# Seven block products instead of eight for the products with A, the last step of LayerNorm on ScalarE, and eight groups in flight

## The chip, the cores and the metric

The kernel runs on one core of one Trainium2 chip. The metric is the device time of one execution in microseconds (us), the median of several runs.

A core has TensorE (PE, matrix products; its weight loads are shown as PEld), VectorE (DVE), ScalarE (ACT), GpSimd (POOL) and a queue that issues DMAs (SP). The engines work side by side, each in its own order, and wait for one another through semaphores. Matrix products read SBUF and write PSUM, of which the kernel uses eight banks of 128 x 512 f32 numbers.

## The reference

x is 64 batches of 256 nodes with 128 features, and A a dense 256 x 256 matrix, all in f32. Four layers run one after another, each as LN(x + layer(x)); LN has no scale or shift.

```python
# layer 0: y = sum over k of X_k W_k with X = x, Ax, AAx, AAAx, Ax, AAx, AAAx
# layer 1: A (x W) + b
# layer 2: An x W^T + b,   An = D^-1/2 (A + I) D^-1/2
# layer 3: five steps of a gated unit
m_in = jnp.einsum('nm,bmd->bnd', in_matrix, h)      # in_matrix = out_matrix = A
z = jax.nn.sigmoid(av @ w3_w.T + w3_b + u3)         # av = [A h, A h]
r = jax.nn.sigmoid(av @ w4_w.T + w4_b + u3)         # u3 = h @ u3_w.T + u3_b
hv = jnp.tanh(av @ w5_w.T + w5_b + (r * h @ u5_w.T + u5_b))
h = (1.0 - z) * h + z * hv
```

## The kernel before

**Tiling.** Two batches make a group (`NB = 2`): 31 groups of two and two groups of one batch at the end (`ONES`). A group's x is one tile of 128 x 512: for each of two batches two node tiles of 128, and 128 features for each. A group runs through all four layers by itself; nothing passes between groups.

**Products with A.** `propagate` (L457) computes h^T A^T for one group: for each batch and each half of the nodes one matmul of 128 x 128 (h, stationary) with 128 x 256 (a row half of A^T), four matmuls in one bank, and then ScalarE copies the bank into SBUF (`copied`, L417). It is called for layer 0 with AA (`q`, bank pmq), for layers 1 and 2 (bank pm) and for each of the five steps (bank pmg). In steps 1 to 4 h comes back through DRAM in another layout (`packed`, `pair_of`).

**LayerNorm.** `statistics` (L422): four BN statistics on VectorE, four aggregations, variance + eps (ve), and one GpSimd operation for the power -1/2 (rs). `normalise` (L446): VectorE computes (s - mean) * rs for each of the four 128-wide parts. For layers 1 and 2 GpSimd adds the bias to y (yb, L595).

**Order.** The kernel writes no order by hand. Each `Group.add` hands an operation with an engine, a cost, a lag and a rank to `Plan`; `Plan.order` (L80) lays all of them out by a greedy list schedule over costs, in which an operation takes its place when its inputs and its slots (banks, SBUF tiles, DRAM buffers) are expected to be free, and among those that can start first the one of the lowest rank. The rank is the group's number; for the last `LEVEL` groups the ranks lie close together and grow with the operation's place in the group. The result is a fixed instruction order for each engine. `ACTIVE` is how many groups may be under way: a group's operations come after the last one of the group `ACTIVE` places ahead of it. Costs decide nothing but the order; what waits on the chip is decided by the real times.

**Start.** `WARM` transposes of the identity run on TensorE until A has arrived. A is transposed, squared, and normalised for layer 2; weights are summed and transposed. The first `HEAD` batches are transposed by TensorE, all later ones by a VectorE block transpose and a way through DRAM (tx, dx, xT).

```python
def propagate(self, tag, h, aTs, ins=None, outs=None):
    ...
            for b in range(self.nb):
                for kt in range(T):
                    mm(o[b], a(h, b * T + kt), aTs.ap[:, kt, :], kt == 0, kt == T - 1)
    ...
    return self.copied("m" + tag, ps)
```

Of the kernel before, what the change touches and what calls it, by code (L numbers as in the profile page):

```python
# [8 lines left out]
F32 = mybir.dt.float32  # L9
AF = mybir.ActivationFunctionType  # L10
# [5 lines left out]
ACTIVE = 6  # L16
HEAD = 4
LEVEL = 6
END = 8
STEPS = 5  # L20
WARM = 12
# [5 lines left out]
class Val:  # L27
# [3 lines left out]
    def __init__(self, kind, shape, name, nb=NB):  # L31
        self.kind, self.shape, self.name, self.nb = kind, shape, name, nb
        self.writer, self.readers, self.users = None, [], []
        self.slot = self.tile = None
# [15 lines left out]
class Plan:  # L50
# [9 lines left out]
    def add(self, engine, cost, lag, rank, run, reads=(), writes=(), after=()):  # L60
        if engine == "SP":
            lag += 700
        op = Op(len(self.ops), rank, engine, cost, lag, run, [*reads, *writes])
        op.deps.update(after)
        for v in reads:
            op.deps.add(v.writer)
            v.readers.append(op)
        for v in writes:
            if v.writer is not None:
                op.deps.add(v.writer)  # L70
            op.deps.update(v.readers)
            v.writer, v.readers = op, []
        op.deps.discard(op)
        for v in op.vals:
            if op not in v.users:
                v.users.append(op)
        self.ops.append(op)
        return op
# [66 lines left out]
def dve_cost(elements):  # L145
    return elements / 0.96 + 75


def act_cost(elements):
    return elements / 1.2 + 165  # L150
# [3 lines left out]
def kernel(  # L154
# [42 lines left out]
    SHAPES = {"bank": [P, 512], "x": [P, 512], "w": [P, 512], "st": [P, Q * 6], "mv": [P, Q * 2],  # L197
              "ve": [P, Q], "rs": [P, Q]}
    slots = {"bank": BANKS, "x": ACTIVE + 3, "w": 54, "dram1": 8, "dram2": 16, "st": 8, "mv": 8, "ve": 8, "rs": 8}
# [3 lines left out]
    def constant(name, shape):  # L203
        v = Val("const", shape, name)
        v.tile = const.tile(shape, F32, name=name)
        return v
# [8 lines left out]
    def load(rank, name, shape, src):  # L215
        v = constant(name, shape)
        pre(rank, "SP", 450, lambda: nc.sync.dma_start(v.ap, src), [], [v])
        return v
# [11 lines left out]
    def warmed():  # L230
        for i in range(WARM):
            nc.tensor.transpose(warm.ap[:, (i % 4) * P:(i % 4 + 1) * P], ident, ident)  # L232
# [4 lines left out]
    a_nat = load(-9, "a_nat", [P, T, N], adj.rearrange("(t p) m -> p t m", p=P))  # L237
# [12 lines left out]
    pre(-8, "PE", 4 * 110, lambda: turn(p_at, a_nat), [a_nat], [p_at])  # L250
# [42 lines left out]
    ahat, anT = constant("ahat", [P, T, N]), constant("anT", [P, T, N])  # L293
# [24 lines left out]


    w1s = load(1.3, "w1s", [P, C], w1)  # L320
    b1s = load(1.4, "b1s", [P, C], bass.AP(tensor=b1.tensor, offset=b1.offset, ap=[[0, P], [1, C]]))
    raw = {name: load(1.5, f"raw_{name}", [P, src.shape[1]], src)
           for name, src in (("w2", w2), ("w4", w4_w), ("w3", w3_w), ("w5", w5_w), ("u3", u3_w), ("u5", u5_w))}
    b2s = load(1.5, "b2s", [P, C], bass.AP(tensor=b2.tensor, offset=b2.offset, ap=[[0, P], [1, C]]))
    both = {name: constant(f"both_{name}", [P, C]) for name in ("w4", "w3", "w5", "w34")}
# [32 lines left out]
    def nat(v):  # L358
        return v.ap.rearrange("p (q c) -> p q c", c=C)
# [7 lines left out]
    def tile_of(v, q):  # L367
        return nat(v)[:, q, :]

    def pair_of(v, q):  # L370
        return v.ap.rearrange("p (b c t) -> p b t c", c=C, t=T)[:, q // T, q % T, :]
# [8 lines left out]
    class Group:  # L380
# [15 lines left out]
        def rank(self):  # L396
            g = self.start / NB
            return g if g < G - LEVEL else G - LEVEL + (g - G + LEVEL) / 10 + self.count / 100

        def add(self, engine, cost, lag, run, reads=(), writes=()):  # L400
            after = () if self.first else self.gate
            self.count += 1
            op = plan.add(engine, cost, lag, self.rank(), run, reads, writes, after)
            self.first = self.first or op
            self.last = op
            return op

        def pe(self, cost, run, reads, writes):
            return self.add("PE", cost, 260, run, reads, writes)

        def dve(self, run, reads, writes, cost=None):
            return self.add("DVE", cost or dve_cost(self.width), 260, run, reads, writes)

        def act(self, run, reads, writes, cost=None):
            return self.add("ACT", cost or act_cost(self.width), 130, run, reads, writes)
# [6 lines left out]
        def statistics(self, tag, s):  # L422
            st, mv, ve, rs = (self.val(k, k + tag) for k in ("st", "mv", "ve", "rs"))

            def stats():
                for q in range(self.q):
                    nc.vector.bn_stats(st.ap[:, q * 6:(q + 1) * 6], nat(s)[:, q, :])  # L427

            def aggr():
                for q in range(self.q):  # L430
                    nc.vector.bn_aggr(mv.ap[:, 2 * q:2 * q + 2], st.ap[:, q * 6:(q + 1) * 6])  # L431
                nc.vector.tensor_scalar(ve.ap, mv.ap.rearrange("p (q k) -> p q k", k=2)[:, :, 1], EPS,  # L432
                                        None, op0=OP.add)

            self.dve(stats, [s], [st], 195 * self.q)
            self.dve(aggr, [st], [mv, ve], 67 * self.q + 142)
            self.add("POOL", 1010, 100,
                     lambda: nc.gpsimd.tensor_tensor(rs.ap, ve.ap, half[:, :self.q], op=OP.pow), [ve], [rs])  # L438
            return mv, rs
# [6 lines left out]
        def normalise(self, tag, s, mv, rs):  # L446
            y = self.val("w", "y" + tag)

            def run():
                for q in range(self.q):  # L450
                    nc.vector.tensor_scalar(nat(y)[:, q, :], nat(s)[:, q, :], mv.ap[:, 2 * q:2 * q + 1],  # L451
                                            rs.ap[:, q:q + 1], op0=OP.subtract, op1=OP.mult)

            self.dve(run, [s, mv, rs], [y], 257 * self.q)
            return y

        def propagate(self, tag, h, aTs, ins=None, outs=None):  # L457

            ps = self.val("bank", "pm" + tag)

            def run():
                o, a = (outs or plain)(ps), ins or tile_of
                for b in range(self.nb):
                    for kt in range(T):
                        mm(o[b], a(h, b * T + kt), aTs.ap[:, kt, :], kt == 0, kt == T - 1)

            self.pe(pe_cost(N, self.q), run, [h, aTs], [ps])
            return self.copied("m" + tag, ps)

# [62 lines left out]
        def record(self):  # L532
# [23 lines left out]
            qT = self.propagate("q", x_, a2T)  # L556
# [3 lines left out]
            for t in range(T):  # L560
                p = self.val("bank", f"py0{t}")
                py.append(p)

                def first(p=p, t=t):
                    for b in range(self.nb):
                        o, q = p.ap[:, b * 2 * C:(b + 1) * 2 * C], b * T + t
                        mm(o, (tile_of if near else pair_of)(xT, q), w01.ap[:, 0:2, :], b == 0, True, shared=True)
                        mm(o, tile_of(qT, q), w0s.ap[:, 2:4, :], False, True, shared=True)

                def moved(p=p, t=t):  # L570
                    nc.scalar.copy(parts(v)[:, t], four(p)[:, :, 1, :])

                self.pe(pe_cost(2 * C, 2 * self.nb), first, [xT, qT, w01, w0s], [p])
                self.act(moved, [p], [v], act_cost(self.nb * C))
            for t in range(T):

                def second(p=py[t], t=t):
                    for kt in range(T):
                        mm(four(p)[:, :, 0, :], aT.ap[:, kt, t * P:(t + 1) * P], parts(v)[:, kt],
                           False, True, shared=True)  # L580

                def summed(p=py[t], t=t):
                    nc.vector.tensor_copy(nat(s0).rearrange("p (b t) c -> p t b c", t=T)[:, t],
                                          four(p)[:, :, 0, :])

                self.pe(pe_cost(self.nb * C, T), second, [v, aT], [py[t]])
                self.dve(summed, [py[t]], [s0], dve_cost(self.nb * C))
# [25 lines left out]
            for s in range(STEPS):  # L613
                m = self.propagate(f"g{s}", h, ats, ins, by_block)
# [14 lines left out]
                if s < STEPS - 1:  # L629
                    hT = self.tensor(f"hT{s}", OP.add, hT, e)  # L630
                    h, ats, ins = self.packed(f"h{s}", hT), aTp, pair_of
# [31 lines left out]
    with tc.manual_schedule():  # L663
        for op in plan.order():
            for v in op.vals:
                if v.tile is None:
                    pool = {"bank": psum_b, "dram1": dram, "dram2": dram}.get(v.kind, sbuf)
                    v.tile = pool.tile(v.shape, F32, tag=f"{v.kind}{v.slot}", name=v.name)
            op.run()
# [30 lines left out]
```

## Time and profile before

| | |
|---|---|
| median of 3 runs | 1382.38 us (1381.41 to 1382.77) |
| profiled execution: its own time / its span | 1382.45 us / 1380.7 us |
| TensorE clock granted, mean over the span | 0.998 |
| matmul passes / VectorE / ScalarE / GpSimd instructions | 5044 / 2735 / 833 / 205 |
| DMA | 134.08 MB, mean 97 GB/s |

The span runs from the first to the last instruction of the profiled execution. "Busy" counts the time in which an engine has at least one operation under way. An f32 matmul stands in the profile as two matmul records (two passes), each with its own weight load. Matmuls overlap with the next one, so a record's length is more than the time that it holds the engine. A group of instructions is named by line, engine and operation, and by what it writes and reads (out<-in).

### The profile page before, as it was taken

The numbers are of one execution on the slowest core, as the hardware profiler recorded it, in microseconds if no ns is written. First come the engines' busy times: TensorE is split into PE (matmuls) and PEld (weight loads), VectorE is DVE, ScalarE is ACT, GpSimd is POOL, SyncE is SP. The second block draws the span as 40 slices with busy tenths as digits, with TensorE's granted clock in tenths as the row PEclk, the third lists the DMA queues.
The fourth block names the chain that finished last, engine by engine and source line by source line (L and its number), as shares of the span: only waits on it lengthen the run. The fifth ranks groups of instructions, "written<-read, shape, count | busy, mean of one in ns | idle before, by whom it ended". The sixth has DMA issues, their size and how long they took to land.

```text
span 1380.7 us, 16602 instructions
## 1 busy us (share of the span) xinstructions
PE 1366.5 (99%) x5044; PEld 922.5 (67%) x5044; DVE 970.5 (70%) x2735; ACT 513.1 (37%) x833; POOL 236.1 (17%) x205
## 2 busy tenths in 40 slices
PE   9999999999999999999999999999999999999996
PEld 8866666666667766566676666667666677766664
DVE  4755686867667767776686767668685778875577
ACT  2233433333433233433424333442334332334443
POOL 1400021202111211011121211012221113210001
PEclk9999999999999999999999999999999999999999
DMA  6023233333333332343241334333232432233332
GB/s 177 31 77 91 85 115 115 91 98 105 112 107 90 109 92 75 97 137 110 64 137 54 108 108 117 95 92 106 78 107 84 118 97 85 85 92 90 86 103 65
DMA packets 271112, 134.08 MB, mean 97 GB/s; under 512 B 177584, under 2 KB 243632, under 8 KB 271024
## 3 DMA queue, kind: packets, MB, share of 16 engines
q1 hardware_dynamic: 271024, 133.03, 33.2%
q8 instruction: 40, 0.66, 0.2%
q14 instruction: 48, 0.39, 0.1%
HBM read 67.05 MB, written 65.54 MB: 96 GB/s over the span
## 4 chain that ended last, share of the span: by engine, by line
PE 97%; DVE 2%; DMA 0%; ACT 0%; issue 0%; POOL 0%; SPq 0%; POOLq 0%; DVEq 0%
PE pr L195 30%; PE ph L195 19%; PE pmg L195 19%; PE py L195 16%; PE pm L195 8%; PE pmq L195 4%; DVE y L451 1%; DMA h<-dh 0%; DVE st L427 0%; PE p_a L195 0%; PE warm L232 0%; DVE s L443 0%; DVE d L529 0%; DVE mv L431 0%; DVE e L529 0%
## 5 line engine op out<-in xcount | busy, mean ns | idle before, releaser
L195 PE MATMUL pr<-mg,w435u5T 128*128 128x512 f32 (+1 forms) x660 | 323.3, 580 | 1.7 <-ACT mg L419 1.4
L438 POOL TENSOR_TENSOR rs<-ve,half 128x4 f32<-128x4 f32 (+1 forms) x132 | 137.9, 1049 | 1049.8 <-DVE ve L432 1049.7
L529 DVE TENSOR_TENSOR d<-hv,hT 128x512 f32<-128x512 f32 (+1 forms) x165 | 113.6, 690 | 189.6 <-ACT hv L522 189.2
L195 PE MATMUL pmg<-aTp,h 128*128 128x256 f32 x1024 | 241.7, 379 | 0.4 <-DMA h<-dh 0.4
L195 PEld LDWEIGHTS pmg<-aTp,h 128*128 128x128 f32 x1024 | 200.4, 196 | 50.5 <-issue 24.4
L529 DVE TENSOR_TENSOR rh<-r,hT 128x512 f32<-128x512 f32 (+1 forms) x165 | 116.5, 706 | 128.2 <-ACT r L522 126.9
L195 PEld LDWEIGHTS pr<-mg,w435u5T 128*128 128x128 f32 x660 | 123.6, 190 | 101.0 <-issue 90.4
L419 ACT COPY mg<-pmg 128x512 f32<-128x512 f32 (+1 forms) x165 | 94.6, 573 | 257.0 <-PE pmg L195 236.5
L451 DVE TENSOR_SCALAR y<-s,mv,rs 128x128 f32<-128x128 f32 x512 | 149.7, 357 | 34.0 <-POOL rs L438 32.5
L195 PE MATMUL pr<-hT,w2u3T 128*128 128x512 f32 (+1 forms) x330 | 163.1, 580 | 1.1 <-DVE hT L529 1.1
L522 ACT ACTIVATE z<-pr,bsum 128x512 f32<-128x512 f32 (+1 forms) x165 | 111.3, 674 | 142.2 <-PE pr L195 137.4
L195 PE MATMUL ph<-mg,w435u5T 128*128 128x512 f32 (+1 forms) x330 | 163.4, 579 | 0.0
L195 PE MATMUL ph<-rh,w435u5T 128*128 128x512 f32 (+1 forms) x330 | 163.0, 579 | 0.0
L522 ACT ACTIVATE r<-pr,bsum 128x512 f32<-128x512 f32 (+1 forms) x165 | 111.3, 674 | 135.2 <-PE pr L195 132.7
L522 ACT ACTIVATE hv<-ph,bsum 128x512 f32<-128x512 f32 (+1 forms) x165 | 111.3, 674 | 53.0 <-PE ph L195 50.9
L529 DVE TENSOR_TENSOR e<-z,d 128x512 f32<-128x512 f32 (+1 forms) x165 | 113.8, 691 | 2.5
L529 DVE TENSOR_TENSOR hT<-hT,e 128x512 f32<-128x512 f32 (+1 forms) x165 | 113.1, 687 | 2.5
L427 DVE BATCH_NORM_STATS2 st<-s 128x6 f32<-128x128 f32 x512 | 109.7, 277 | 0.8
L195 PEld LDWEIGHTS ph<-rh,w435u5T 128*128 128x128 f32 x330 | 62.4, 190 | 69.3 <-issue 59.5
L195 PEld LDWEIGHTS ph<-mg,w435u5T 128*128 128x128 f32 x330 | 62.4, 190 | 67.5 <-issue 54.8
L504 DVE STREAM_TRANSPOSE th<-hT 128x512 f32<-128x512 f32 x132 | 91.0, 689 | 2.0
L195 PEld LDWEIGHTS pr<-hT,w2u3T 128*128 128x128 f32 x330 | 61.6, 190 | 42.0 <-issue 25.2
(79 smaller groups left out, 1373.7 us busy)
## 6 DMA issues: line engine op xcount, KB each, us to landing
dh<-th SPq DMA_DIRECT2D x155, 256.0 KB, 2.0
h<-dh SPq DMA_DIRECT2D x256, 128.0 KB, 2.5
x<-in_x_dram SPq DMA_DIRECT2D x31, 256.0 KB, 3.3
hT<-dh SPq DMA_DIRECT2D x124, 64.0 KB, 2.0
out_dram<-y SPq DMA_DIRECT2D x31, 256.0 KB, 2.4
xT<-dx SPq DMA_DIRECT2D x60, 128.0 KB, 2.5
dx<-tx SPq DMA_DIRECT2D x29, 256.0 KB, 2.6
dn<-tn SPq DMA_DIRECT2D x28, 256.0 KB, 2.0
```

Source lines behind the costliest of these rows:

```text
L195: nc.tensor.matmul(o, lhsT, rhs, start=start, stop=stop, skip_group_check=shared)
L419: self.act(lambda: nc.scalar.copy(t.ap, ps.ap), [ps], [t])
L427: nc.vector.bn_stats(st.ap[:, q * 6:(q + 1) * 6], nat(s)[:, q, :])
L438: lambda: nc.gpsimd.tensor_tensor(rs.ap, ve.ap, half[:, :self.q], op=OP.pow), [ve], [rs])
L451: nc.vector.tensor_scalar(nat(y)[:, q, :], nat(s)[:, q, :], mv.ap[:, 2 * q:2 * q + 1], rs.ap[:, q:q + 1], op0=OP.subtract, op1=OP.mult)
L504: self.dve(lambda: nc.vector.transpose(turn.ap.rearrange("p (u j t) -> p u t j", t=T, j=32), src.ap.rearrange("p (u t i) -> p u t i", t=T, ...
L522: self.act(lambda: nc.scalar.activation(t.ap, ps.ap, func, bias=bias[1], scale=1.0), [ps, bias[0]], [t], act_cost(self.width) + 100)
L529: self.dve(lambda: nc.vector.tensor_tensor(out(t), way(a), way(b), op=op), [a, b], [t])
```

## The change

- **Seven block products.** With h of two batches taken as a 2 x 2 matrix of 128 x 128 blocks (batch by node half), and A^T as another one, `propagate` now calls `seven` for all full groups before the last `PLAIN` = 10 batches, but not for layer 0 of the first two groups and not for steps 1 to 4. `seven` forms three sums of h's blocks on GpSimd (ts, two operations, and tq, one), does seven matmuls of 128 x 128 in four pieces (`first`, `middle`, `more`, `rest`), and puts the result together with a copy of one block by ScalarE (`kept`), three VectorE additions, another copy by ScalarE and one more VectorE addition. The sums of A^T's blocks are made once at the start (`block_sums`, three times five VectorE operations).
- **LN.** The last step is four ScalarE activations, Identity with scale rs and bias -mean * rs; VectorE makes -mean (nm), and GpSimd a second small operation for the product. Layer 0's sum out of PSUM (s0) goes from VectorE to ScalarE.
- **Order.** `ACTIVE` 6 to 8, `LEVEL` 6 to 4, the rank's growth within a group doubled, more slots (w 54 to 60, and others), some constants moved into the shared slots. VectorE costs in the plan are 6% higher. Several operations may now write one value without being ordered among themselves (`joint`).
- **Start.** `WARM` 12 to 14, and four more warming transposes behind those of A.

```diff
-ACTIVE = 6
+ACTIVE = 8
-LEVEL = 6
+LEVEL = 4
+PLAIN = 10
-WARM = 12
+WARM = 14
...
 def dve_cost(elements):
-    return elements / 0.96 + 75
+    return (elements / 0.96 + 75) * 1.06
...
+    def turned_early():
+        turn(p_at, a_nat)
+        warming(4)
...
+        def run():
+            nc.vector.tensor_add(v.ap[:, 0, :], a21, a22)
+            nc.vector.tensor_sub(v.ap[:, 1, :], v.ap[:, 0, :], a11)
+            nc.vector.tensor_sub(v.ap[:, 2, :], a11, a21)
+            nc.vector.tensor_sub(v.ap[:, 3, :], a12, v.ap[:, 1, :])
+            nc.vector.tensor_scalar(v.ap[:, 4, :], a22, -1.0, None, op0=OP.mult)
...
-            return g if g < G - LEVEL else G - LEVEL + (g - G + LEVEL) / 10 + self.count / 100
+            return g if g < G - LEVEL else G - LEVEL + (g - G + LEVEL) / 10 + self.count / 50
...
+                nc.vector.tensor_scalar(nm.ap, mean, -1.0, None, op0=OP.mult)
+
+            def scales():
+                nc.gpsimd.tensor_tensor(rs.ap, ve.ap, half[:, :self.q], op=OP.pow)
+                nc.gpsimd.tensor_tensor(mv.ap[:, :self.q], nm.ap, rs.ap, op=OP.mult)
...
-                    nc.vector.tensor_scalar(nat(y)[:, q, :], nat(s)[:, q, :], mv.ap[:, 2 * q:2 * q + 1],
-                                            rs.ap[:, q:q + 1], op0=OP.subtract, op1=OP.mult)
-
-            self.dve(run, [s, mv, rs], [y], 257 * self.q)
+                    nc.scalar.activation(nat(y)[:, q, :], nat(s)[:, q, :], AF.Identity, bias=mv.ap[:, q:q + 1],
+                                         scale=rs.ap[:, q:q + 1])
+
+            self.act(run, [s, mv, rs], [y], 400 * self.q)
...
+            if fast and self.nb == 2 and self.start < B - PLAIN:
+                return self.seven(tag, h, aTs, ins or tiles, blocks)
...
+            def ts01():
+                nc.gpsimd.tensor_tensor(ts.ap[:, :2 * P].rearrange("p (x c) -> p x c", x=2), ins(h)[:, 1], ins(h)[:, :, 0],
+                                        op=OP.subtract)
+            def ts2():
+                nc.gpsimd.tensor_tensor(row(ts, 2), ins(h)[:, 1, 1], row(ts, 0), op=OP.subtract)
+            def ts3():
+                nc.gpsimd.tensor_tensor(tq.ap, row(ts, 2), ins(h)[:, 0, 1], op=OP.subtract)
...
+            def first():
+                block(0, ins(h)[:, 0, 0], aTs.ap[:, 0, :P], True)
+            def middle():
+                block(2, row(ts, 0), sums.ap[:, 0, :])
+                block(1, row(ts, 1), sums.ap[:, 2, :])
+                block(3, row(ts, 2), sums.ap[:, 1, :])
+            def more():
+                block(0, ins(h)[:, 0, 1], aTs.ap[:, 1, :P])
+            def rest():
+                block(2, ins(h)[:, 1, 1], sums.ap[:, 3, :])
+                block(1, tq.ap, sums.ap[:, 4, :])
...
+            started = self.pe(pe_cost(P, 1), first, [h, aTs], [ps])
+            kept = self.act(lambda: nc.scalar.copy(row(u, 1), row(ps, 0)), [ps], [u], act_cost(P))
+            self.add("POOL", 830, 100, ts01, [h], [ts])
+            self.add("POOL", 610, 100, ts2, [h, ts], [ts])
+            self.add("POOL", 590, 100, ts3, [h, ts], [tq])
+            self.pe(pe_cost(P, 3), middle, [ts, sums], [ps], True, (started,))
+            self.pe(pe_cost(P, 1), more, [h, aTs], [ps], True, (kept,))
+            self.dve(post11, [ps, u], [u], 215)
+            self.dve(post12, [ps, u], [w], 215)
+            self.dve(post13, [ps, w], [m], 215)
+            self.act(lambda: nc.scalar.copy(o(m, 0), o(ps, 0, False)), [ps], [m], act_cost(P), True)
+            self.pe(pe_cost(P, 2), rest, [h, tq, sums], [ps], True)
+            self.dve(post2, [ps, u], [m], 340, True)
...
-            qT = self.propagate("q", x_, a2T)
+            qT = self.propagate("q", x_, a2T, fast=not near)
...
-                    nc.vector.tensor_copy(nat(s0).rearrange("p (b t) c -> p t b c", t=T)[:, t],
+                    nc.scalar.copy(nat(s0).rearrange("p (b t) c -> p t b c", t=T)[:, t],
...
-                m = self.propagate(f"g{s}", h, ats, ins, by_block)
+                m = self.propagate(f"g{s}", h, ats, ins, True, fast=s == 0)
```

## The prediction

> **What bounds the kernel now.** I read the busy times first, then the chain that ended last, then the stretches, and only then single operations.
>
> ```profile
> PE 1366.5 (99%) x5044; PEld 922.5 (67%) x5044; DVE 970.5 (70%) x2735; ACT 513.1 (37%) x833; POOL 236.1 (17%) x205
> PE 97%; DVE 2%; DMA 0%; ACT 0%; issue 0%; POOL 0%; SPq 0%; POOLq 0%; DVEq 0%
> ```
>
> The first line is busy time by engine, the second the share of each engine in the chain of waits. A busy TensorE alone proves little; that 97% of the chain is TensorE itself, not what it waits for, does. By stretch of the span:
>
> ```profile
> core 0: us, PE busy (x) PEld busy (x) DVE busy (x) ACT busy (x) POOL busy (x), PEclk, DMA share, GB/s
> 20.00:1340.00 1320.00, 1318.99 (x4853) 887.71 (x4852) 933.08 (x2618) 492.50 (x794) 229.90 (x193) 1.00 0.33 97
> 1340.00:1381.00 41.00, 29.55 (x113) 19.16 (x111) 30.85 (x99) 14.11 (x27) 4.83 (x6) 0.93 0.24 68
> ```
>
> From 20 to 1340 us TensorE idles 1.0 us. A microsecond of matmul taken out there is a microsecond of time, as long as nothing else comes late. How long a matmul really holds the engine is seen from starts, since the ends overlap the next one. The timeline of TensorE (start, us, operation, count of passes; an f32 matmul is two passes):
>
> ```profile
> 700.17 1.89 PE L195 MATMUL pm<-aT,y 128*128 128x256 f32 x8
> 701.90 1.89 PE L195 MATMUL pmg<-aTp,h 128*128 128x256 f32 x8
> 703.63 1.05 PE L195 MATMUL py<-w1s,m 128*128 128x128 f32 x8
> 704.52 1.02 PE L195 MATMUL pr<-hT,w2u3T 128*128 128x512 f32 x2
> 705.38 1.02 PE L195 MATMUL pr<-mg,w435u5T 128*128 128x512 f32 x2
> ```
>
> Start to start: 256 columns take 1.73/8 = 0.2164 us a pass, 128 columns 0.89/8 = 0.111, 512 columns 0.86/2 = 0.43. Priced so, the program's matmuls come to 1360.9 us; the other 19.8 us of the 1380.7 us span are the cold clock and gaps of the head and the drain of the end.
>
> [...]passes of 128 columns with a new weight each follow at 111 ns. [...]Rows of yb and of d (duration ns min/median/max), then a stretch of the timeline:
>
> ```profile
> L595 POOL TENSOR_TENSOR yb<-y,b1s x33: 727/1270/4023, 26.6 to 1213.8; 128x512 f32<-128x512 f32 x31, 128x256 f32<-128x256 f32 x2
> L529 DVE TENSOR_TENSOR d<-hv,hT x165: 408/692/1646, 68.1 to 1372.0; 128x512 f32<-128x512 f32 x155, 128x256 f32<-128x256 f32 x10
> ```
>
> ```profile
> 314.43 0.68 DVE L529 TENSOR_TENSOR hT<-hT,e 128x512 f32<-128x512 f32 x1
> 314.65 2.20 POOL L595 TENSOR_TENSOR yb<-y,b2s 128x512 f32<-128x512 f32 x1 [1.93 <-DVE y L451]
> 315.03 0.69 DVE L529 TENSOR_TENSOR rh<-r,hT 128x512 f32<-128x512 f32 x1
> 315.63 0.71 DVE L504 STREAM_TRANSPOSE th<-hT 128x512 f32<-128x512 f32 x1
> ```
>
> yb takes 1.27 us alone and 2.20 us here[...]. In the other direction d took up to 1.65 instead of 0.69 us.
>
> **The change, part by part.**
>
> *Seven blocks for eight.* 27 groups (starts 0 to 52) have layers 1, 2 and step 0, 25 of them also layer 0's product (not groups 0 and 2): 3 x 27 + 25 = 106 products. Each was 4 matmuls of 256 columns, 8 x 0.2164 = 1.731 us; it becomes 7 of 128, 14 x 0.111 = 1.554 us. 106 x 0.177 = 18.8 us off TensorE. [...]I take 0.111, from a run of eight with changing weights.
>
> *New waits on TensorE.* The block matmuls come in four pieces: first, middle (needs ts, two GpSimd operations), more, rest (needs a third one, and three VectorE additions). TensorE works in order, so a late middle holds everything behind it, other groups' gate products too. I priced the changed order with the passes above and measured how much other matmul work stands between first and middle. GpSimd's price is from yb: 512 elements 1.27, 256 0.727, so 2.1 ns an element and 0.18 us: ts01 0.73, ts2 and ts3 0.455 each. Unhindered, ts01 + ts2 take 1.18 us, with hand-overs (0.1) 1.28; with the mean hindrance that yb shows (mean of 512 elements 1.41 and 1.52 against 1.27, about a sixth) 1.5. Between first and middle there is less than 1.28 us of work in 18 of the 106 products, 7.8 us short in all; less than 1.54 in 23, 13.6 us short; less than 2.0 in 38, 26.9 short. These are upper bounds: GpSimd starts when h is there, not when first ends, and first alone takes 0.22 us. I take 4 us. Between more and rest at least 1.5 us stand, against three additions of 0.28 us (the 128x512 one with a PSUM input takes 0.68, 128x128 copies out of PSUM 0.285) and hand-overs: covered. From rest to the use of the product nearly everywhere over 1.1 us against about 0.7 for the last addition: covered.
>
> *VectorE.* Goes: y 149.7, the copies s of layer 0 26.2. Comes: nm 132 x 0.17 = 22, additions 106 x (3 x 0.28 + 0.41) = 133, and blocking by 106 x 1.64 = 174 us of ts operations. What blocking costs VectorE is known only by yb, some 0.2 us for each us of yb: 33 us, between 0 and 60. Sum: 970 - 176 + 155 + 33 = 982 of about 1370 us, 72% as against 70%. Not a bound, but no relief either. I charge 2 us of TensorE for gate operations that come late in this way.
>
> *ScalarE.* Goes: 106 copies of 0.587 = 62. Comes: two 128-column copies each (373 ns for 256 columns, so 0.27) = 57, layer 0's copies 66 x 0.37 = 24, y 512 x 0.38 = 195 (a 128-column copy 0.27, and 0.1 for each pointer operand by the gates' 687 against the copies' 587 ns; overlap takes some off; between 0.33 and 0.47). 513 + 214 = 727 us, 53%. [...]the changed program has one load as before. y is no slower than on VectorE (1.11 us for four, now about 1.5), with one GpSimd step (0.4) more: 0.8 us more in a chain of over 5, which has 6.8 us of matmuls or more beside it everywhere.
>
> *GpSimd.* 236 + 174 unhindered (215 with hindrance) + 132 x 0.4 = about 500 us, 37%.
>
> *Eight in flight, slots.* The longer chains (some 3 us a product) are paid by 8 groups instead of 6. A product's bank is held longer, 49 us in the mean for layer 0 and 11 to 14 for the others in the priced order, which is 1.7 of the eight banks at a time. Nothing on the path.
>
> *Head.* Before, TensorE ran cold until about 10 us (p_a's eight passes start at 5.71 and what follows at 9.29, 0.45 us a pass), with a gap before p_a. Four transposes now fill this gap. [...]1.5 us are gained (p_a: 3.58 us, warm 1.73); two more warming transposes cost 0.4. Against that, four layer-0 products are begun one after the other before group 0 goes on, the fourth needs the fourth far load of x, which before was issued at 20.76 and there at 24.7 us, and GpSimd works off their ts before group 0's rs: a hold of about 1.5 us. I set the head at +0.4.
>
> *End.* The last five full groups and both single ones keep eight products. The last normalisation gets nm (0.17), a GpSimd step (0.4) and 0.2 for ScalarE: +0.8. The new ranks reorder the last 40 us by an unknown +/-2.
>
> Sum: -18.8 + 4 + 2 + 0.4 + 0.8 = -11.6. The profiled execution took 1382.45 us (span 1380.7), the median of the runs is 1382.38, so the same base: 1371.
>
> **The rivals.**
>
> *B, all of it arrives.* The waits were counted too high, the clock comes early: 1382.4 - 18.8 - 1.5 + 1.2 = 1363. For it: 1.0 us idle in 1320 now, in an order worked out the same way. Against: 18 short places.
>
> *C, fill and drain eat it.* In the first 100 us every product lies on few groups' chains (seven of the 23 short places are there), and from 1340 us VectorE is already 75% busy. 18 us lost at both ends: 1382.
>
> *D, slower[...].* [...]yb shows what a GpSimd operation can meet: 4.0 and 4.7 us at worst. If from the end of first the ts chain needs 2.5 us in the mean, 45 middles are short by 47 us; with a third of that covered by an early start, 31 stay: 1382.4 - 18.8 + 31 = 1394. It decides from a need of about 1.7 us (18.4 us short). [...]Against: y leaves VectorE[...].
>
> **How the numbers follow.** Forecast 0.50 (1364.5 to 1379), B 0.15, C 0.13, D 0.22. About 0.2%, 2.8 us, is what a measurement of this kernel can tell from no change. Faster: 0.50 + 0.15 + 0.04 of C = 0.69; same 0.06; slower 0.22 + 0.03 = 0.25. The range, 1360 to 1388, takes in B, C and the mild part of D.
>
> **What would show it.** Right: TensorE's chain share stays over 93%, its 128-column passes at 0.111 us, 106 x 7 x 2 = 1484 of them more, waits of middle on ts of a few us in all, d and hT a few per cent longer, VectorE near 980 us. Wrong: waits of the pm matmuls on GpSimd over 15 us, ts operations over 1 us in the mean (D); gaps only before 100 and after 1300 us (C); 128-column passes over 0.12 us.

## The result, and the profile after

| | before | after |
|---|---|---|
| median | 1382.58 us (1381.41 to 1382.82, 4 runs) | 1381.27 us (1381.08 to 1383.17, 4 runs) |
| ratio | | 0.9995, 95% interval 0.9978 to 1.0013 |
| profiled execution: its own time / its span | 1382.45 / 1380.7 us | 1383.17 / 1380.9 us |
| mean TensorE clock granted | 0.998 | 0.994 |

No change that can be measured; 1371 us was forecast. The page of after, busy time by engine and the shares of the chain of waits:

```profile
PE 1357.5 (98%) x5686; PEld 931.4 (67%) x5686; DVE 942.6 (68%) x2728; ACT 710.2 (51%) x1517; POOL 459.0 (33%) x655
PE 91%; DVE 4%; ACT 1%; DMA 1%; issue 1%; SPq 1%; POOL 1%; ACTq 0%; POOLq 0%; DVEq 0%
```

TensorE has less to do and is waited for less: its share of the chain fell from 97 to 91%, and VectorE took 4%, although VectorE was busy for 28 us less than before. The stretches of after tell where:

```profile
core 0: us, PE busy (x) PEld busy (x) DVE busy (x) ACT busy (x) POOL busy (x), PEclk, DMA share, GB/s
20.00:60.00 40.00, 37.81 (x230) 34.65 (x229) 21.49 (x96) 18.32 (x57) 29.14 (x47) 0.96 0.45 124
200.00:400.00 200.00, 196.22 (x833) 135.15 (x833) 142.81 (x419) 102.53 (x223) 76.69 (x109) 0.99 0.36 103
400.00:600.00 200.00, 196.15 (x825) 132.61 (x824) 139.08 (x394) 102.78 (x219) 77.66 (x106) 0.99 0.34 100
600.00:800.00 200.00, 199.96 (x870) 137.48 (x869) 142.50 (x428) 104.89 (x231) 75.21 (x107) 1.00 0.34 98
```

Two things are new: idle TensorE (2 to 4 us in three of these stretches) and PEclk below 1.00 in the same three. Busy time hides short waits. So, for each matmul pass, the distance from its start to the next start was taken, less the price of such a pass (0.111, 0.2164 and 0.4295 us for 128, 256 and 512 columns). The sum of what is over is called excess below; it holds idle gaps and passes made slow by the clock alike:

| kernel | passes at their price | excess 0-20 us | 20-60 | 60-1340 | 1340-end |
|---|---|---|---|---|---|
| before | 1360.8 | 4.8 | 0.0 | 0.4 | 6.8 |
| after | 1342.7 | 3.1 | 4.4 | 17.8 | 4.8 |

So the passes brought 18.1 us, the very start 1.7 and the end 2.0; 4.4 us went at 20 to 60 us and 17.4 in the body (60 to 1340 us). It cancels; the two spans differ by 0.2 us. The body's 17.8 us in after are two gaps of over 2 us (5.3 us), the half clock behind them (3.4 us) and some 70 gaps of under 1 us (9.1 us). The waits of TensorE's matmuls in after, by line and releaser (us in total, times, longest):

```profile
PE pth L591 <- DVE hT L645: 3.3, 2, 2.2
PE pr L199 <- DVE mq L569: 2.7, 1, 2.7
PE pm L199 <- DVE m L565: 2.6, 2, 2.3
PE pmq L199 <- DMA x<-in_x_dram: 2.2, 2, 1.9
```

The first is the drain. The other three are mainly single long waits: at 23.9 us for the x of a far group (one whose x is turned by way of DRAM), at 234 us for mq, at 592 us for m. No line names GpSimd except for the identity at the start. The timeline of after around 234 us, TensorE, then VectorE, then GpSimd (start, us, operation; in brackets the idle time before it and its releaser):

```profile
233.83 0.39 PE L199 MATMUL pm<-aT,y 128*128 128x128 f32 x2
236.91 1.18 PE L199 MATMUL pr<-hT,w2u3T 128*128 128x512 f32 x2 [2.70 <-DVE mq L569]
237.89 0.63 PE L199 MATMUL pmg<-s_aT,y 128*128 128x128 f32 x2
238.32 0.63 PE L199 MATMUL pmg<-s_aT,tqg 128*128 128x128 f32 x2
```

```profile
229.75 0.24 DVE L565 TENSOR_TENSOR mq<-wsq,pmq 128x128 f32<-128x128 f32 x1
229.97 0.71 DVE L645 TENSOR_TENSOR d<-hv,hT 128x512 f32<-128x512 f32 x1
230.60 1.22 DVE L481 TENSOR_TENSOR s<-hn,y 128x512 f32<-128x512 f32 x1
231.74 0.94 DVE L645 TENSOR_TENSOR e<-z,d 128x512 f32<-128x512 f32 x1
232.60 0.86 DVE L461 BATCH_NORM_STATS2 st<-s 128x6 f32<-128x128 f32 x4
233.38 1.39 DVE L645 TENSOR_TENSOR hT<-hT,e 128x512 f32<-128x512 f32 x1
...
236.36 0.41 DVE L569 TENSOR_TENSOR mq<-pmq,usq 128x256 f32<-128x256 f32 x1
```

```profile
230.09 1.18 POOL L531 TENSOR_TENSOR ts<-y 128x256 f32<-128x256 f32 x1
231.35 0.78 POOL L535 TENSOR_TENSOR ts<-y,ts 128x128 f32<-128x128 f32 x1
...
232.96 1.27 POOL L711 TENSOR_TENSOR yb<-y,b1s 128x512 f32<-128x512 f32 x1
```

pr, a gate product, does not read mq. It takes the bank that layer 0's product of another group holds until the last of its four additions (in the kernel's plan, the group of batch 6 takes it from that of batch 16), and that addition starts on VectorE 6.6 us behind the third. On the way s, e and hT, which take 0.68 us alone, took 1.22, 0.94 and 1.39, s and e beside the new sums ts, hT beside the bias addition yb, which the kernel before has too. After the wait two 128-column passes take 0.43 us instead of 0.22: the clock granted from 237.8 to 241.2 us was 0.50. At 592 us it is `rest` that waits, for the third addition:

```profile
592.17 0.39 PE L199 MATMUL pm<-aT,y 128*128 128x128 f32 x2
594.84 0.49 PE L199 MATMUL pm<-s_aT,y 128*128 128x128 f32 x2 [2.28 <-DVE m L565]
```

### The profile page after: what moved, and what is told of

The parts are those of the page before. It is cut to its first block, busy times and chain, and to the rows that moved or that the text cites. A ratio compares the mean times of both kernels' runs of the same rounds, so it can differ in the third digit from the quotient of the medians.

```text
span 1380.9 us, 18955 instructions
## 1 busy us (share of the span) xinstructions
PE 1357.5 (98%) x5686; PEld 931.4 (67%) x5686; DVE 942.6 (68%) x2728; ACT 710.2 (51%) x1517; POOL 459.0 (33%) x655
## 4 chain that ended last, share of the span: by engine, by line
PE 91%; DVE 4%; ACT 1%; DMA 1%; issue 1%; SPq 1%; POOL 1%; ACTq 0%; POOLq 0%; DVEq 0%
PE pr L199 28%; PE pmg L199 19%; PE ph L199 18%; PE py L199 15%; PE pm L199 7%; PE pmq L199 3%; DMA x<-in_x_dram 1%; ACT y L489 1%; DVE e L645 1%; DVE hT L645 1%; DVE d L645 1%; DVE s L481 0%; DVE st L461 0%; POOL rs L471 0%; DVE rh L645 0%
## 5 line engine op out<-in xcount | busy, mean ns | idle before, releaser
L471 POOL TENSOR_TENSOR rs<-ve,half 128x4 f32<-128x4 f32 (+1 forms) x132 | 142.6, 1080 | 765.1 <-DVE nm L468 764.0
L489 ACT ACTIVATE y<-s,mv,rs 128x128 f32<-128x128 f32 x512 | 210.2, 484 | 21.6 <-POOL mv L472 20.8
L645 DVE TENSOR_TENSOR rh<-r,hT 128x512 f32<-128x512 f32 (+1 forms) x165 | 123.1, 750 | 114.6 <-ACT r L638 112.4
L199 PEld LDWEIGHTS pr<-mg,w435u5T 128*128 128x128 f32 x660 | 120.2, 190 | 93.2 <-issue 80.5
L452 ACT COPY mg<-pmg 128x512 f32<-128x512 f32 (+1 forms) x138 | 78.4, 569 | 162.1 <-PE pmg L199 160.3
L645 DVE TENSOR_TENSOR hT<-hT,e 128x512 f32<-128x512 f32 (+1 forms) x165 | 116.5, 711 | 2.0
L620 DVE STREAM_TRANSPOSE th<-hT 128x512 f32<-128x512 f32 (+1 forms) x132 | 90.2, 687 | 1.2
```

Source lines behind the costliest of these rows:

```text
L199: nc.tensor.matmul(o, lhsT, rhs, start=start, stop=stop, skip_group_check=shared)
L452: self.act(lambda: nc.scalar.copy(t.ap, ps.ap), [ps], [t])
L489: nc.scalar.activation(nat(y)[:, q, :], nat(s)[:, q, :], AF.Identity, bias=mv.ap[:, q:q + 1], scale=rs.ap[:, q:q + 1])
L620: self.dve(lambda: nc.vector.transpose(turn.ap.rearrange("p (u j t) -> p u t j", t=T, j=32), src.ap.rearrange("p (u t i) -> p u t i", t=T, ...
L645: self.dve(lambda: nc.vector.tensor_tensor(out(t), way(a), way(b), op=op), [a, b], [t])
```

## The experiments

Theory "waits": seven blocks save their 18 us on TensorE, and these go again because an in-order TensorE waits for VectorE in tight places, the long waits with a stretch of half clock behind them. Rivals: VectorE's operations that run long beside GpSimd's (of d, e, hT and rh with 128x512 in after, the 503 that no ts, tq or yb overlaps took 0.64 to 0.73 us, the other 117 0.94 us in the mean and up to 1.77); the other parts of the change; the amount of work on the engines whatever the order.

**x1_short_read: the reads of GpSimd's sums.** This asks whether the late VectorE operations before 234 and 592 us come from the sums beside them. GpSimd's three sums read only 8 of 128 columns, and memsets fill the rest, so the products with A are incomplete; the order is that of after. The edit of the second sum (the other two likewise):

```diff
-                nc.gpsimd.tensor_tensor(row(ts, 2), ins(h)[:, 1, 1], row(ts, 0), op=OP.subtract)
+                nc.gpsimd.tensor_tensor(row(ts, 2)[:, :8], ins(h)[:, 1, 1, :8], row(ts, 0)[:, :8], op=OP.subtract)
+                nc.gpsimd.memset(row(ts, 2)[:, 8:], 0.0)
```

> The three sums of h's blocks on GpSimd read and write 8 of 128 columns and fill the rest with zeros without reading (the products with A are so left incomplete); the order of all engines stays as in the changed kernel. [...]both TensorE gaps of over 2 us and both half-clock stretches behind them go, and most of the small gaps between 200 and 600 us: 1369 to 1373 us. Rival 'order': VectorE's additions stand too far back in its queue[...]: within 2 us of 1381.

Measured: 1375.56 us, ratio to before 0.9947 (0.9932 to 0.9962). Body excess 10.9 instead of 17.8 us: the wait at 234 us shrank to 2.16 us and kept its half clock, the one at 590 us fell to 1.29 and lost it. Neither forecast came (1369 to 1373, or 1381): some 6 us of the loss go when these sums hardly read, the rest does not. Before 234 us s and e are back at 0.70 and 0.68 us, while hT takes 1.57, still beside yb.

**x2_head_order: the head.** The fourth far group's tx, ts01 and `first` are moved behind group 0's statistics and scales and the second matmuls of group 2's layer 0. The core of the edit (the lines around it apply the new places):

```diff
+        for late, behind in ((find("DVE", "tx_10"), find("DVE", "mv0_0", "aggr")),
+                             (find("POOL", "tsq_10", "ts01"), find("POOL", "mv0_0", "scales")),
+                             (find("PE", "pmq_10", "first"), second)):
+            late.start = behind.start + 0.5
...
```

> Order changed in the head alone: the first block matmul, the first sum and the transpose of the fourth far group go behind group 0's statistics and scales and behind group 2's layer 0. Theory 'head wait': TensorE's gap of 2.1 us at 23.8 us and the half clock behind it (1.7 us) go, later gaps stay: 1377 to 1378 us. Rival: group 0's own chain ends as late, so that the gap only moves: within 1 us of 1381.

Measured: 1384.09 us, ratio 1.0009 (1.0000 to 1.0018), slower than both forecasts. TensorE's wait for the fourth far x is gone, and a gap of 2.5 us stands at 29.5 us, with half clock behind it. At 20 to 60 us the excess is 6.3 us. The new gap's chain, in order of time:

```profile
29.74 0.71 DVE L661 STREAM_TRANSPOSE tx<-x 128x512 f32<-128x512 f32 x1 [3.44 <-DMA x<-in_x_dram]
31.12 0.28 DVE L559 TENSOR_TENSOR usq<-usq,pmq 128x128 f32<-128x128 f32 x1
31.75 0.29 ACT L572 COPY us<-pm 128x128 f32<-128x128 f32 x1
32.08 0.49 PE L199 MATMUL pm<-aT,y 128*128 128x128 f32 x2 [2.35 <-ACT us L572]
```

VectorE stood still for the next far x, whose DMA was issued at 24.59 us. Behind it in VectorE's order stood the addition usq; behind a copy that needs usq, in ScalarE's order, stood the copy us, and TensorE needed us. So the wait for a late x did not go, it moved to another engine's queue.

**x4_no_seven: the change without its first part.** `PLAIN = 64`, so that every product keeps its eight blocks; all the rest as after.

> All products with eight blocks (PLAIN = 64), everything else as changed: LN's last step on ScalarE, eight in flight, the new costs, ranks and start. Theory: these parts are neutral in the stretch from 60 to 1340 us, TensorE has no gap there, the head and the end bring 1 to 4 us: 1378 to 1382 us. Rival 'the rest of the change costs time': over 1386 us, and the seven blocks bring their 18 us after all.

Measured: 1383.80 us, ratio 1.0008 (1.0000 to 1.0017), between the forecasts (1378 to 1382, over 1386) and nearer to the first. The body excess is 1.9 us (of an execution of 1382.22 us), the one at 20 to 60 us 1.3; the body has one gap of 2.66 us, at 1225 us, for LN's last step (y) on ScalarE. LN on ScalarE, eight in flight, more slots and the new start are together worth about +1 us. So the 17 us of the body are lost only with seven blocks.

**x5_ln_vector: seven blocks without LN on ScalarE.** The last step of LN goes back to VectorE, in the plan too, so that the order changes with it.

```diff
-                    nc.scalar.activation(nat(y)[:, q, :], nat(s)[:, q, :], AF.Identity, bias=mv.ap[:, q:q + 1],
-                                         scale=rs.ap[:, q:q + 1])
+                    nc.vector.tensor_scalar(nat(y)[:, q, :], nat(s)[:, q, :], rs.ap[:, q:q + 1],
+                                            mv.ap[:, q:q + 1], op0=OP.mult, op1=OP.add)
```

> Seven blocks, but LN's last step on VectorE as before (one multiply-add instruction of the same shape). Theory: VectorE gets 150 us of work back[...]: more gaps of over 2 us, 1388 to 1400 us. Rival 'VectorE's load is not what counts': within 3 us of 1381.

Measured: 1387.03 us, ratio 1.0030 (1.0018 to 1.0042); VectorE 1093 us busy, 16% of the chain. The time is 1 us under the forecast 1388 to 1400. Body excess 20.3 us, but not in the way expected: no gap reaches 2 us (five have 1 to 2 us), no stretch of half clock stands there, and 13 us are gaps of under 1 us. With seven blocks, LN on VectorE costs some 5 us more than on ScalarE. With eight blocks the move to ScalarE brought nothing that shows (x4_no_seven, together with the other parts).

**x6_ladder: what a single wait costs.** The kernel before, with k GpSimd multiplications by 1 of h ahead of one product of five groups.

```diff
+            stalls = {12: 3, 20: 4, 28: 5, 36: 6, 44: 7}.get(self.start, 0) if tag == "g2" else 0
             def run():
...
+                for _ in range(stalls):
+                    nc.gpsimd.tensor_scalar(h.ap, h.ap, 1.0, None, op0=OP.mult)
```

> The kernel before, with 3, 4, 5, 6 and 7 GpSimd multiplications by 1 put ahead of step 2's product of the groups 12, 20, 28, 36 and 44, on the h that it reads, so that TensorE stands still there for a time that grows from one place to the next. Theory 'clock': a single gap of over about 2 us is followed by one stretch of 3.4 us at half clock, which costs 1.7 us more[...]; the time is before's plus all gaps plus 1.7 us for each long one. Rival: the half clock after the three gaps of after is chance, or needs more than one gap: gaps of 2 to 5 us without it, and the time is before's plus the gaps alone.

TensorE's timeline at the first place, and stretches around the first three of the ladder (the number before DMA share is the clock):

```profile
323.31 1.89 PE L195 MATMUL pm<-anT,y 128*128 128x256 f32 x8
327.95 3.65 PE L195 MATMUL pmg<-aTp,h 128*128 128x256 f32 x8 [2.75 <-POOL h L466]
331.40 1.10 PE L195 MATMUL pr<-hT,w2u3T 128*128 128x512 f32 x2
```

```profile
324.00:332.00 8.00, 5.25 (x16) 3.78 (x15) 4.45 (x7) 1.11 (x3) 3.73 (x3) 0.79 0.35 105
510.00:525.00 15.00, 8.45 (x30) 6.51 (x29) 7.52 (x36) 1.76 (x3) 11.46 (x9) 0.77 0.44 123
640.00:655.00 15.00, 8.65 (x23) 5.62 (x22) 4.48 (x7) 2.33 (x4) 6.65 (x4) 0.77 0.24 72
```

After a gap of 2.91 us eight passes of 256 columns take 3.45 us from start to start instead of 1.73. The five gaps are 2.91, 6.71, 6.51, 6.70 and 11.43 us, 34.3 in all, and the passes behind them lose 1.8, 1.8, 2.8, 2.9 and 1.6 us, nearly all of it at half clock. Together 45.2 us, against 1427.22 - 1382.27 = 45.0 measured (a single run). So half clock followed gaps that were put in by hand too, and cost 1.6 to 2.9 us at each. No gap under 2.9 us was tried, and the four longer ones show two or three stretches of 3.41 us at half clock and not one, part of them in the gap itself.

**x7_lag200 and x8_slow_plan: the same instructions in another order.** Only numbers that `Plan` counts with are changed.

```diff
x7_lag200, and in x8_slow_plan too (ts2 and ts3 likewise):
-            self.add("POOL", 830, 100, ts01, [h], [ts])
+            self.add("POOL", 830, 200, ts01, [h], [ts])
...
x8_slow_plan alone (VectorE's lag 260 to 320 too, post12 and post13 as post11, post2 340 to 410):
-    return (elements / 0.96 + 75) * 1.06
+    return (elements / 0.96 + 75) * 1.12
-            self.dve(post11, [ps, u], [u], 215)
+            self.dve(post11, [ps, u], [u], 260)
```

> The same instructions as after; only the plan counts 200 instead of 100 ns from the end of each of the three GpSimd sums (ts01, ts2, ts3) to their use, so that middle and rest are placed later in TensorE's order. Theory 'order': the 18 us of gaps come from an order that leaves the block products too little room, and half or more of them go: 1364 to 1372 us, no TensorE gap over 2 us between 60 and 1200 us and no half-clock stretch there. Theory 'engines': the waits follow from the amount of work on VectorE and GpSimd[...], and another order of the same work only moves them: 1377 to 1385 us.

> The same instructions; the plan counts the GpSimd sums' lag as 200 ns, VectorE's operations 12 instead of 6% higher, their lag 320 instead of 260 ns, and the additions after the seven products at 260 and 410 instead of 215 and 340 ns. Theory 'order': 1362 to 1370 us, the excess of TensorE's starts over the pass prices between 60 and 1200 us at 3 to 8 us (after: about 17). Theory 'engines': 1377 to 1385 us.

Measured: x7_lag200 1373.04 us, ratio 0.9932 (0.9915 to 0.9948); x8_slow_plan 1373.72, ratio 0.9938 (0.9923 to 0.9952). The body's excess is 8.4 us in both, and neither has a half-clock stretch there (each has one before 40 us). They end 1 and 3.7 us above what "order" expected and well outside "engines": some 8 us of the loss belong to the order, though the engines do the same work. What went is of the size of the two long waits and their half clock (8.7 us in after); the small gaps, 9.1 us in after, still make up nearly all of the 8.4.

**x9_no_layer0: layer 0 as before.** `fast=False` for the product with AA.

> Layer 0's product keeps its eight block products in all groups; layers 1, 2 and step 0 have seven. This gives up 25 of 106 products, 25 x 0.177 = 4.4 us of TensorE, and takes away the banks that are held for some 50 us until their last VectorE addition, and a quarter of the GpSimd sums. Theory 'order' (with the bank as one of its waits): the gap at 234 us and its half-clock stretch are gone, the excess falls by 8 to 13 us, and 1368 to 1376 us come out although less is saved on TensorE. Theory 'engines': waits in proportion to the products, a quarter of 18 us less against 4.4 us given up: 1380 to 1383 us.

Measured: 1370.88 us, ratio 0.9918 (0.9903 to 0.9932), with no wait over 2 us and no half clock before the drain. The passes cost 1347.1 us (4.4 more than after), the body's excess is 3.2 us (14.6 less). The 25 products of layer 0 cost three times what they save in after's order. Since leaving them out also reorders everything else, this alone does not show that it was the bank.

**x12_lag_short: are the sums' reads dear in any order?** x7_lag200's order, with the short reads of x1_short_read. What is asked is how much of the 6 us that these reads cost in after they cost here.

> The order of x7_lag200 (GpSimd lag 200 ns in the plan), and as in x1_short_read GpSimd's three sums read only 8 of 128 columns and fill the rest by memset[...]; the result is then not the reference's. Theory 'tight places': [...]in an order with room at these places it costs 0 to 2.5 us: 1370.5 to 1373. Rival[...]: it costs the same 6 us in any order, since the same sums block the same VectorE operations: 1366 to 1368.

Measured: 1372.83 us, ratio 0.9927 (0.9910 to 0.9944), against 0.9932 for x7_lag200. The same removal that was worth 6 us in after is worth less than 1 us here. So what these reads cost depends on the order. In after, half of it was paid at the two long waits (1.9 us of gap, 1.7 of half clock), the rest in small gaps.

**x10_tuned and x11_tuned_no0: plans with more room.** Their numbers leave more time to VectorE and to the GpSimd sums; x10_tuned keeps seven blocks in layer 0 (102 products), x11_tuned_no0 does not (81).

```diff
x10_tuned (VectorE's lag 260 to 300 too, post12 and post13 as post11, post2 340 to 450, ts2 and ts3 as ts01):
-PLAIN = 10
+PLAIN = 12
-    return (elements / 0.96 + 75) * 1.06
+    return (elements / 0.96 + 75) * 1.1
-            return self.add("PE", cost, 260, run, reads, writes, joint, behind)
+            return self.add("PE", cost, 300, run, reads, writes, joint, behind)
-            self.add("POOL", 830, 100, ts01, [h], [ts])
+            self.add("POOL", 830, 250, ts01, [h], [ts])
-            self.dve(post11, [ps, u], [u], 215)
+            self.dve(post11, [ps, u], [u], 300)
...
x11_tuned_no0 (ts2 and ts3 as ts01):
-    return (elements / 0.96 + 75) * 1.06
+    return (elements / 0.96 + 75) * 1.14
-            self.add("POOL", 830, 100, ts01, [h], [ts])
+            self.add("POOL", 830, 150, ts01, [h], [ts])
-            qT = self.propagate("q", x_, a2T, fast=not near)
+            qT = self.propagate("q", x_, a2T, fast=False)
```

> Seven blocks in layers 0, 1, 2 and step 0 up to batch 52 (102 products, worth 102 x 0.177 = 18.1 us), planned with more room: GpSimd sums' lag 250 ns, VectorE costs +10% and lag 300, TensorE's lag 300, additions at 300 and 450 ns. Theory 'order': fewer gaps than x7_lag200, 1366 to 1371 us. Rival 'bank': as long as layer 0's products hold their banks for some 50 us, any order leaves gaps in the body, and it does not get under x9_no_layer0: 1371 to 1376 us.

> Layer 0 with eight block products everywhere, seven in layers 1, 2 and step 0, and the plan with VectorE costs +14% and 150 ns lag of the GpSimd sums. Theory 'order': the body's excess (60 to 1300 us), 3.3 us in x9_no_layer0, goes to about 1 us: 1368 to 1370.5 us. Rival: what is left in x9_no_layer0 lies at the head and the end, which no number of the plan touches: 1370.5 to 1372 us.

Measured: x10_tuned 1369.74 us, ratio 0.9907 (0.9893 to 0.9922); x11_tuned_no0 1369.27, ratio 0.9899 (0.9884 to 0.9914), which beats both kernels by about 1%; the two can't be told apart. Page and stretches of x11_tuned_no0:

```profile
PE 1352.0 (99%) x5536; PEld 926.2 (68%) x5536; DVE 911.9 (67%) x2628; ACT 710.2 (52%) x1492; POOL 413.7 (30%) x580
PE 96%; DVE 1%; DMA 1%; SPq 1%; issue 0%; ACT 0%; POOL 0%; ACTq 0%; POOLq 0%; DVEq 0%
```

```profile
20.00:60.00 40.00, 36.81 (x213) 32.58 (x212) 19.98 (x86) 18.76 (x53) 23.11 (x34) 1.00 0.45 124
200.00:400.00 200.00, 200.00 (x833) 138.53 (x832) 136.03 (x403) 105.43 (x227) 66.76 (x95) 1.00 0.36 104
400.00:600.00 200.00, 200.00 (x819) 134.41 (x818) 136.79 (x382) 106.42 (x224) 70.01 (x96) 1.00 0.34 98
```

From 60 to 1340 us the excess is 0.4 us, as in the kernel before: 81 x 0.177 = 14.3 us saved arrive there in full. x10_tuned, with 102 products and layer 0's long-held banks, has a body excess of 5.0 us and is no slower than x9_no_layer0 (rivals' 1371 to 1376 us did not come): a held bank does not forbid a good order. What neither took away is the 3 to 4 us at 20 to 60 us, without a half clock there in either.

| kernel | passes at their price | excess 0-20 us | 20-60 | 60-1340 | 1340-end | median |
|---|---|---|---|---|---|---|
| after | 1342.7 | 3.1 | 4.4 | 17.8 | 4.8 | 1381.27 |
| x1_short_read | 1342.7 | 3.5 | 4.2 | 10.9 | 4.9 | 1375.56 |
| x5_ln_vector | 1342.7 | 2.9 | 4.7 | 20.3 | 5.7 | 1387.03 |
| x7_lag200 | 1342.7 | 3.4 | 4.3 | 8.4 | 4.8 | 1373.04 |
| x9_no_layer0 | 1347.1 | 2.3 | 3.1 | 3.2 | 4.8 | 1370.88 |
| x10_tuned | 1343.4 | 3.1 | 3.5 | 5.0 | 4.9 | 1369.74 |
| x11_tuned_no0 | 1347.1 | 2.8 | 4.2 | 0.4 | 4.8 | 1369.27 |

## Why the prediction was wrong

- **Seven blocks, -18.8 us: right.** Passes at 0.111 us, 636 more of them (106 x 6) and six warming ones; -18.1 us with these.
- **The wait of middle on GpSimd, 4 us: not there.** TensorE's matmuls in after wait for GpSimd nowhere in the body, so the late middles of rival D did not occur either. The sums did get longer, as these two groups of after show (mean ns behind the busy time; unhindered 730 and 455), but the plan had put middle late enough:

```profile
L531 POOL TENSOR_TENSOR ts<-y 128x256 f32<-128x256 f32 x54 | 48.8, 905 | 3.2 <-DVE nm L468 1.9 <-PE pm L199 1.0 <-PE pmq L199 0.3
L535 POOL TENSOR_TENSOR ts<-y,ts 128x128 f32<-128x128 f32 x54 | 28.9, 537 | 2.2
```

- **"Between more and rest at least 1.5 us stand ...: covered" and banks "Nothing on the path": the step that failed.** I compared the matmuls in between with three additions' own durations, as if VectorE were free for them. In its order gate operations, s and st of other groups stand between the additions (gate operations ahead of the third at 592 us; 6.6 us from the third to the fourth before 234 us), and those among them that run beside GpSimd's sums or yb take longer (up to 1.39 us instead of 0.68 before 234 us). I also priced VectorE's lateness at 2 us for gate operations alone, and gave the bank held by layer 0's product a mean (1.7 of 8 banks) where the one bank that is next in turn counts. The two long waits that come of it and the clock behind them are 8.7 us of the body. The other 9.1 us are small gaps, which went with other plans (x9, x10, x11); they were not followed one by one.
- **The plan had these holes.** `Plan.order` of after, laid out by its own costs, leaves TensorE idle ahead of the same pr for 1.96 us and ahead of the same rest for 1.06 us; x1_short_read, where the sums hardly read, had gaps of 2.16 and 1.29 there, after of 2.86 and 2.44. From 60 to 1320 us of the plan the holes sum to 0 us in before, 11.5 in after, 10.7 in x7_lag200, 7.6 in x10_tuned, and 1.7 and 1.9 in x9_no_layer0 and x11_tuned_no0. They are a warning and no forecast: x5_ln_vector has 9.6 and lost 20.3.
- **The clock: no term at all.** In after's profile three gaps of 2.1 to 2.9 us (7.4 us) are each followed by 3.41 us at half clock, 1.7 us more each, 5.1 in sum: 12.5 of the 22.2 us of excess between 20 and 1340 us. I counted the clock at the start only. The other three executions of after have mean clocks of 0.995 to 0.996, where the profiled one has 0.994, and take 2 us less. That they had fewer such stretches is likely, but they were not profiled.
- **Head, +0.4: right in kind, wrong in size.** The earlier clock came (full from 5.7 instead of 10.2 us; p_a's passes follow at 0.216 instead of 0.427 us) and gave 1.7 us for the 1.5 counted, which was an estimate of mine. The hold by the fourth far x, set at 1.5 us, is 2.1 us of wait, 1.7 of half clock and 0.6 of small waits. That the clock's 1.7 us would be saved here is not shown: x12_lag_short had the same gap as x7_lag200 (2.15 us) without the half clock, and its excess at 20 to 60 us is 4.2 us against 4.3.
- **End, +0.8: the wrong sign.** The last 40 us have 2.0 us less excess.
- **Engine loads: too high, and beside the point.** VectorE 943 us (982 forecast), ScalarE 710 (727), GpSimd 459 (500). The 0.4 us for a small GpSimd step was an estimate; the new one (mv) took 0.20. VectorE was less busy than before and cost more.
- **Rival C** had the right time, 1382 us, by the wrong places: 17.4 of the lost us lie in the body, 4.4 at the fill, none at the drain.

Shown: the saving arrives on TensorE; the body's loss needs seven blocks (x4_no_seven); half of it goes in another order of the same instructions (x7, x8), most of it in an order for four products fewer (x10), so the amount of work does not force it; what GpSimd's reads cost depends on the order (x1 against x12); half clock followed gaps of 2.9 us and more that were put in by hand (x6). Open: what stands behind each of the small gaps, and which single number of the plan is to blame. The lag of the GpSimd sums was raised in all of x7, x8, x10 and x11, but each number reorders the whole list, so this doesn't show that this lag is the wrong one. No run has seven blocks with the ranks and the six groups in flight of before. Whether the head's 3 to 4 us can go with seven blocks was not tried beyond x2_head_order.

## What to carry to other kernels

A change that splits one product into pieces with other engines in between needed here not a faster or freer engine so much as an order with room: ask for each new wait what stands ahead of its releaser in that engine's own order, and not how long the releaser takes. When a saving on the bounding engine doesn't arrive, change the order with the instructions kept (a lag in the planner is enough) before blaming bandwidth or engines that slow one another. Where a planner lays out the order, look first at the holes in its own layout. And a TensorE gap of 2 to 3 us may cost 1.7 us more by the clock: all three of after did, one of 2.24 us in x10_tuned and one of 2.66 us in x4_no_seven did not.

## What was unexpected of the hardware

In after's profile the changes of the granted clock lie whole multiples of 3.413 us apart: it is full from 5.69 us, at half for 3.41 us each from 26.2, 237.8 and 596.2 us (62 and 105 such steps apart), and at half from 1374.4 us to the end. The two changes in before, at 10.2 and 1375.6 us, are 400 steps apart. With after cut into these steps, TensorE's idle time (start-to-start excess of over 0.2 us each) was 2.52, 2.53 and 2.06 us in the steps just ahead of the three half stretches; in every other step between 15 and 1345 us, the half stretches left out, it was at most 1.08 us.

The length of a gap alone did not tell: after's gap of 2.44 us, with 2.06 us of it in one step, had half clock behind it; x4_no_seven's gap of 2.66 us, two steps of which had 1.78 and 1.43 us of idle time (other waits with it), had none. x7_lag200 and x12_lag_short share an order and a gap of 2.15 us at 24 us: in x7_lag200 it lay in one step, and half clock followed at 27.4 us (mean clock of the execution 0.996); in x12_lag_short at most 1.95 us of idle time lay in one step, and none followed (0.997). So a gap of this size cost 1.7 us more in one execution and nothing in another. By what the clock is set is not shown by these few cases. Such differences may be one reason why executions of one kernel differ by about as much; that is not shown either, since one execution of each was profiled.
